# Four edits to a four-layer graph kernel: q and k stored whole and parted between the attention's steps, the nearest row taken in place, the norm rows on four row groups, h times the last weights ahead

## The chip, the core and the metric

The kernel runs on one core of one Trainium2 chip. Its time is the device time of one execution in microseconds (us). TensorE is called PE (PEld is its weight load), VectorE DVE, ScalarE ACT, GpSimd POOL; SP is the engine that here issues nearly all DMAs. L494 is line 494 of the kernel before.

## What is computed

x is 3327 x 128, adj a 3327 x 3327 matrix of zeros and ones (about 16 ones in a row). Each of four layers adds to x a function of h = relu(layernorm(x)):

```python
# layer 0: two rounds of message passing
x1 = swish((adj @ h) @ W + b);  out = swish((adj @ x1) @ W + b)
# layer 1: attention with 128 heads of 8 elements
q = (h @ Wq.T).reshape(128, n, 8); k, v likewise
a = softmax(einsum('dnh,dmh->dnm', q, k) * scale + adj + adj, axis=2)
out = einsum('dnm,dmh->dnh', a, v).reshape(n, 1024) @ Wo.T
# layer 2: a message and a GRU cell
out = gru(relu((adj @ h) @ W_msg.T + b_msg), h)
# layer 3: lap(A, y) = d * (A @ (d * y)) with d = 1/sqrt(row sums of A)
z = leaky_relu(lap(adj, h) @ W1 + b1, 0.1)
S = exp(-sqrt(squared distances of the rows of z) / 2)   # 4 largest of a row kept
out = lap(S + adj, h) @ W2 + b2
```

In `reshape(128, n, 8)` the flat index of a row's 1024 projected elements decides the head, so 26 consecutive rows of h hold one head.

## The kernel before, in words

Node n lies in partition n // 26 and slot n % 26 (T = 26 slots, 3327 = 128 x 26 - 1). The stages follow one another; outside the attention each engine's order is that of the program.

**Layer 0 (0 to 378 us).** Two products of adj, loaded from DRAM in 26 tiles, in float32.

**Projections (378 to 641 us).** For each of 26 blocks of 128 rows, PE forms q, k and v (L404, L415). ACT writes the rounded part of q and k (L409, `hi`, a type in which TensorE multiplies fast), DVE the rest (L410, `lo` = full - `hi`) and the largest magnitude (L411), and SP stores both parts to the DRAM tensors qt and kt (16 rows: 8 of `hi`, 8 of `lo`) and v to vd (L394). After block 1, `load_heads` issues the 28 loads of group 0.

**Attention (641 to 10,592 us).** The columns (queries) come in 7 chunks of 476, the heads in 32 groups of 4, the rows (keys) in 26 steps t. A step of a chunk and a group:

- PE multiplies k by q for four heads on four 32-row groups (L494). Even steps: three results for DVE ("early", 4 buffers), one for ACT ("late"). Odd steps: two and two. PE adds adj to the late ones (L497).
- DVE adds adj to each early one (L499) into p8, the tile of a pair of steps (3 buffers). ACT takes exponentials of the late ones (L500) and, at odd steps, of five results of both steps at once (L504). POOL multiplies one result by exp of adj at odd steps (L502).
- PE weighs v with the results of four steps earlier (L511). After a group DVE copies the sums out (L520) and SP stores them (L523).

At step 4 `load_heads` issues the loads of the next group's k, q and v: 8 of k (208 KB each, 16 partitions), 16 of q, 4 of v. From step 13 on, POOL casts one pair of key slots a step, 13 in all (`key_pair`, L373). At step 22 tiles of adj for the next chunk are loaded, doubled on POOL (L270) and stored as bfloat16. The order on every engine is the program's, under `manual_schedule`:

```python
scores(step, heads, a_t[t], e_t[t // 2], p8)
...
if j >= ahead:
    weigh(*begun.pop(j - ahead))
if t == min(4, T // 2) and more:
    coming = load_heads(*groups[n])
if t >= T // 2 and more:
    key_pair(coming)
```

**Output projection and layer 2 (10,592 to 10,856 us).** `adj_matmul_parts` (L228) multiplies adj in bfloat16 by three parts of y (its sum in bfloat16), 26 tiles of 21 matmuls; the tiles come through a pool of 4 that is opened for each product. Beside the first product PE transposes h (L646).

**Layer 3 (10,856 to 11,391 us).** A second product with adj gives z (L718 to L728). For each of 26 tiles PE forms the negative distances (L774) and adds the norms as products with K = 3 (L777: `one_rows` x `n_rows`, both on partitions 0 to 2), ACT evacuates (L778), DVE finds the eight largest (L779) and their indices (L780). `second` turns these, in pieces of 4, 9 and 13 tiles, into d2, weights `sim`, and y = h * d2 / 2, splits y and stores it to yd. A third product with adj runs beside the gathers: per tile POOL gathers four rows of yd (L791), DVE sums them by weight (L798, L800), PE transposes the sum (L805). At the end two float32 products with W2 per tile (L822, L823), two DVE operations per quad of tiles (L825, L826) and the stores (L829).

A flag n_gen, formed after the projections from the largest magnitudes and the low bits of adj, decides whether an exact and much slower version of the attention and of all that follows runs afterwards (`For_i` over n_once); for these inputs it is 0.

Of the kernel before, what the change touches and what calls it, by code (L numbers as in the profile page):

```python
# [8 lines left out]
F32 = mybir.dt.float32  # L9
F32R = mybir.dt.float32r  # L10
# [10 lines left out]
P = 128  # L21
# [5 lines left out]
E = 8  # L27
# [26 lines left out]
def kernel(  # L54
# [56 lines left out]
    deg = const.tile([P, T], F32, name="deg")  # L111
    a_max = const.tile([P, T], F32, name="a_max")
# [21 lines left out]
    def in_pieces(f):  # L134

        todo = [slice(t0, t1) for t0, t1 in zip(CUTS, CUTS[1:]) if t1 > t0]

        def done(t):
            while todo and todo[0].stop <= t:
                p = todo.pop(0)  # L140
                f(p, p.stop - p.start)

        return done
# [47 lines left out]
    def adj_matmul(agg, lhs, on_tile=None, bufs=3):  # L191

        cs = chunks(N, 512)
        with tc.tile_pool(name="adj_ps", bufs=1, space=PSUM) as ps, tc.tile_pool(name="adj_in", bufs=bufs) as ap:
# [23 lines left out]
    def adj_matmul_parts(agg, parts, on_tile=None):  # L218

        cs = chunks(N, 512)  # L220
        with tc.tile_pool(name="adj_ps", bufs=1, space=PSUM) as ps, tc.tile_pool(name="adj_in", bufs=4) as ap:
            acc = [ps.tile([P, 512], F32, name=f"agg_ps{c}") for c in range(len(cs))]
            for t in range(T):
                a = ap.tile([P, N], BF16, name="a16")
                nc.sync.dma_start(a, adj16[t])
                for i, part in enumerate(parts):
                    for c, (c0, w) in enumerate(cs):
# [5 lines left out]
                            stop=(t == T - 1 and i == 2),  # L233
# [39 lines left out]
    with tc.tile_pool(name="l0", bufs=1) as pool:  # L273
# [46 lines left out]
        fix = pool.tile([P, 1], F32, name="fix")  # L320
        nc.gpsimd.affine_select(fix, ones, pattern=[[0, 1]], compare_op=ALU.is_gt, fill=0.0, base=P - 1, channel_multiplier=-1)
        nc.vector.tensor_scalar(fix, fix, -1.0, 1.0, op0=ALU.mult, op1=ALU.add)
        nc.vector.tensor_add(deg[:, T - 1 : T], deg[:, T - 1 : T], fix)
# [4 lines left out]

    kt = dpool.tile([HL, GP], F32, name="kt")
# [15 lines left out]

    def load_heads(c, g):
        q0, _ = q_chunks[c]
        we = even(c)
        k_in = kq.tile([P, NP], F32, name="k_in", bufs=1)
        q4 = kq.tile([P, QW], F32R, name="q4")  # L350
        v4 = kq.tile([P, 4, T, EA], F32, name="v4")
        for i in range(4):
            n0 = (4 * g + i) * N
            for j in range(2):
                r = 32 * i + HL * j
                nc.sync.dma_start(k_in[r : r + HL], kt[:, n0 : n0 + NP])
                for k in range(2):
                    nc.sync.dma_start(
                        q4[r + E * k : r + E * k + E, :we].bitcast(F32),
                        qt[E * j : E * j + E, n0 + q0 : n0 + q0 + we],  # L360
                    )
# [14 lines left out]
    with tc.tile_pool(name="l1", bufs=1) as pool, tc.tile_pool(name="l1_ps", bufs=3, space=PSUM) as ps:  # L376
# [6 lines left out]
        for tail in (qt, kt):  # L383
            nc.gpsimd.dma_start(tail[:, N * NH :], zero)
# [12 lines left out]
        assert 3 * N + NP <= P * NH  # L397
        for r in range(T):
            kp = rows_of(r)
            lhs = hT[:, r * P : r * P + kp]  # L400
            for i, (dst, mx) in enumerate(((qt, q_max), (kt, k_max))):
# [3 lines left out]
                scale = D**-0.5 if i == 0 else 1.0  # L405
                s = st.tile([P, 2, E * NH], F32R, name="qk_st")
                full = pp[:kp].rearrange("p a b -> p (a b)")
                hi = s[:kp, 0].bitcast(F32)
                nc.scalar.activation(s[:kp, 0], full, AF.Copy, scale=scale)  # L409
                nc.vector.scalar_tensor_tensor(s[:kp, 1], full, scale, hi, op0=ALU.mult, op1=ALU.subtract)  # L410
                nc.vector.tensor_reduce(mx[:kp, r : r + 1], hi, AX.X, ALU.max, apply_absolute_value=True)  # L411
                store(dst.rearrange("e (r c) -> r e c", c=NH), s.bitcast(F32).rearrange("p a (e c) -> p (a e) c", c=NH), r, kp)
# [7 lines left out]
            if r == 1:  # L420
                first = load_heads(0, 0)
                while len(first[3]) < T // 2:
                    key_pair(first)
                e_first = [exp_of(a, 0) for a in a_first[1::2]]
# [15 lines left out]
        general = pool.tile([P, 1], F32, name="general")  # L440
# [515 lines left out]
```

## Time and profile before

| | |
|---|---|
| median of 3 runs | 11409.84 us (11403.6 to 11420.41) |
| the profiled execution, its span | 11392.72 us, 11391.0 us |
| PE, ACT, DVE, POOL busy | 97%, 90%, 83%, 50% of the span |
| granted PE clock, mean | 0.991 of full |
| DMA | 889.80 MB, 78 GB/s in the mean |
| attention, first L494 to last | 621.1 to 10,585.8 us |
| a group of the attention | 44.2 us (583 L500 in 990 us, one a step) |
| last add of the output (L826) ends | 11382.1 us |

A line of a group gives line, engine, operation, output<-input, shapes, count, busy us, mean ns of one, then the engine's idle time just before these instructions and what ended it. A line of a timeline gives start, length, engine, line, operation, and in brackets the idle time before it and its releaser. A line of windows gives, for a stretch, its length, the busy time of PE, PEld, DVE, ACT and POOL with their counts, then the granted PE clock, the DMA engines' share and GB/s. Instructions of one engine can overlap in the records, so a group's busy time may be less than count times mean.

### The profile page before, as it was taken

The numbers are of one execution on the slowest core, as the hardware profiler recorded it, in microseconds if no ns is written. First come the engines' busy times: TensorE is split into PE (matmuls) and PEld (weight loads), VectorE is DVE, ScalarE is ACT, GpSimd is POOL, SyncE is SP. The second block draws the span as 40 slices with busy tenths as digits, with TensorE's granted clock in tenths as the row PEclk, the third lists the DMA queues.
The fourth block names the chain that finished last, engine by engine and source line by source line (L and its number), as shares of the span: only waits on it lengthen the run. The fifth ranks groups of instructions, "written<-read, shape, count | busy, mean of one in ns | idle before, by whom it ended". The sixth has DMA issues, their size and how long they took to land. (4 is left out here: it accounts for less than half of the span.)

```text
span 11391.0 us, 212068 instructions
## 1 busy us (share of the span) xinstructions
PE 11065.1 (97%) x80100; PEld 3098.6 (27%) x80100; DVE 9408.1 (83%) x15508; ACT 10238.7 (90%) x9182; POOL 5727.5 (50%) x6218
## 2 busy tenths in 40 slices
PE   9789999999999999999999999999999999999998
PEld 4322222222222222222222222222222222222554
DVE  8678888888888888888888888888888888888555
ACT  0379999999999999999999999999999999999332
POOL 0135555555555555555555555555555555555103
PEclk9899999999999999999999999999999999999999
DMA  7853444444444444444444444444443434444423
GB/s 268 244 122 60 70 62 67 64 62 69 61 69 63 63 68 61 69 63 63 67 61 69 63 61 67 61 68 63 62 68 60 68 57 58 58 57 59 138 79 114
DMA packets 476579, 889.80 MB, mean 78 GB/s; under 512 B 91863, under 2 KB 423112, under 8 KB 439962
## 3 DMA queue, kind: packets, MB, share of 16 engines
q1 hardware_dynamic: 470952, 864.64, 43.5%
q8 instruction: 633, 10.37, 0.5%
q0 software_dynamic: 4592, 11.50, 0.3%
q14 instruction: 402, 3.29, 0.1%
HBM read 763.30 MB, written 112.46 MB: 77 GB/s over the span
## 5 line engine op out<-in xcount | busy, mean ns | idle before, releaser
L499 DVE TENSOR_TENSOR p<-early,a 128x476 f32<-128x476 f32 (+1 forms) x14560 | 8435.6, 644 | 1419.7 <-PE early L494 1192.3
L504 ACT ACTIVATE p<-p 128x2380 f32<-128x2380 f32 (+1 forms) x2912 | 6757.4, 2321 | 14.2 <-DVE p L499 0.5
L511 PE MATMUL acc<-p,v 128*9 128x476 f32 (+1 forms) x46592 | 5879.6, 564 | 33.4 <-POOL p L502 13.6
L502 POOL TENSOR_TENSOR p<-p,e 128x476 f32<-128x476 f32 (+1 forms) x2912 | 3539.2, 1215 | 3296.0 <-ACT p L500 3259.4
L500 ACT ACTIVATE p<-late 128x476 f32<-128x476 f32 (+1 forms) x5824 | 4529.2, 897 | 38.9 <-DMA vd<-v_st 20.3
L494 PE MATMUL early<-q,k 32*128 32x476 f32 (+1 forms) x14560 | 2882.9, 477 | 18.8 <-DVE p L499 18.8
L494 PE MATMUL late<-q,k 32*128 32x476 f32 (+1 forms) x8736 | 2797.3, 478 | 62.7 <-ACT p L500 36.3
L373 POOL CAST k<-k_in 128x256 fp32r<-128x256 f32 x2912 | 1946.7, 703 | 1162.5 <-DMA q<-qt 582.7
L494 PEld LDWEIGHTS late<-q,k 32*128 32x128 f32 x8736 | 1065.4, 181 | 4769.9 <-ACT p L500 3241.0
L497 PE MATMUL late<-a,two_i 128*128 128x476 bf16 (+1 forms) x5824 | 2181.0, 374 | 0.0
L494 PEld LDWEIGHTS early<-q,k 32*128 32x128 f32 x14560 | 1144.9, 181 | 23.9 <-DVE p L499 19.5
L511 PEld LDWEIGHTS acc<-p,v 128*9 128x9 f32 x46592 | 710.6, 88 | 1406.4 <-issue 1185.1
L497 PEld LDWEIGHTS <-two_i 128*128 128x128 bf16 x5824 | 556.3, 96 | 1327.5 <-issue 1327.5
L187 ACT COPY agg<-agg_ps 128x512 f32<-128x512 f32 x15 | 8.2, 590 | 476.7 <-PE agg_ps L201 289.7
L228 PE MATMUL agg_ps<-a,part 128*128 128x512 bf16 (+1 forms) x1638 | 338.0, 368 | 18.1 <-DMA a<-adj 13.7
L270 POOL TENSOR_SCALAR a<-a_in 128x476 bf16<-128x476 f32 (+2 forms) x156 | 222.2, 1424 | 0.5
L228 PEld LDWEIGHTS <-part 128*128 128x128 bf16 x1638 | 161.7, 99 | 188.6 <-DVE d_half L759 13.7
L409 ACT ACTIVATE qk_st<-pp 128x1024 fp32r<-128x1024 f32 (+1 forms) x52 | 53.3, 1024 | 149.0 <-DMA qt<-qk_st 67.4
L270 POOL TENSOR_SCALAR a<-a 128x476 bf16<-128x476 f32 (+1 forms) x26 | 36.4, 1400 | 295.3 <-DMA a<-in_adjT_dram 295.3
L778 ACT ACTIVATE dist<-sp,nsq 128x2048 f32<-128x2048 f32 (+1 forms) x52 | 85.5, 1647 | 109.8 <-PE sp L777 100.8
L774 PE MATMUL sp<-yT,hT 128*128 128x512 f32 (+1 forms) x364 | 168.2, 603 | 3.6 <-ACT hT L726 2.1
L201 PE MATMUL agg_ps<-a,h 128*128 128x512 f32 (+2 forms) x364 | 147.4, 568 | 24.3 <-DVE h L162 24.3
(192 smaller groups left out, 2520.2 us busy)
## 6 DMA issues: line engine op xcount, KB each, us to landing
k_in<-kt SPq DMA_DIRECT2D x1792, 208.0 KB
v<-vd SPq DMA_DIRECT2D x896, 117.0 KB
a<-in_adjT_dram SPq DMA_DIRECT2D x50, 1663.5 KB
a<-adj SPq DMA_DIRECT2D x78, 831.8 KB
q<-qt SPq DMA_DIRECT2D x3072, 14.9 KB
a_in<-in_adjT_dram SPq DMA_DIRECT2D x125, 238.0 KB
qt<-qk_st SPq DMA_DIRECT2D x25, 1024.0 KB
kt<-qk_st SPq DMA_DIRECT2D x25, 1024.0 KB
```

The costliest lines, as they stand in the source:

```text
L201: nc.tensor.matmul(acc[c][:, :w], lhs[:kp, t, :], a[:kp, c0 : c0 + w], start=(t == 0), stop=(t == T - 1))
L228: nc.tensor.matmul(acc[c][:, :w], part[:, t, :], a[:, c0 : c0 + w], start=(t == 0 and i == 0), stop=(t == T - 1 and i == 2),)
L270: nc.gpsimd.tensor_scalar(a2[:kp, :w], a, 2.0, None, op0=ALU.mult)
L373: nc.gpsimd.tensor_copy(k, slots(k_in)[:, t : t + 2, :])
L494: nc.tensor.matmul(sp[:, :we], pairs[t // 2][r, t % 2, :], q4[r, :we], start=True, stop=ways[i] != "I")
L497: nc.tensor.matmul(late[:, i - n_d, :we], two_i, a2[:, :we], start=False, stop=True)
L499: nc.vector.tensor_tensor(p8[:, places[i], :we], early[i][:, :we], a2[:, :we], op=ALU.add)
L500: nc.scalar.activation(p8[:, places[n_d] : places[3] + 1, :we], late[:, :, :we], AF.Exp)
L502: nc.gpsimd.tensor_tensor(p8[:, places[3], :we], p8[:, places[3], :we], e_a[:, :we], op=ALU.mult)
L504: nc.scalar.activation(p8[:, :5, :we], p8[:, :5, :we], AF.Exp)
L511: nc.tensor.matmul(acc[32 * i : 32 * i + EA, :w], v4[:kp, i, t, :], p8[:kp, PLACES[t % 2][i], :w], start=(t == 0), stop=(t == T - 1),)
L774: nc.tensor.matmul(sp[:, c0 : c0 + w], slots(zT)[:, t, :], z2T[:, cols], start=True, stop=False)
```

## The change

**q and k.** The projections store q and k whole, in float32, to qf and kf (8 rows each); `hi` and `lo` are no longer formed there. A new class `Parting` reads a group's q and k back (as 96 partitions of 1109), casts to `hi` on POOL in four pieces, subtracts on DVE in four pieces, and stores both to kt and qt. Groups 0 and 1 are parted between the blocks of the projections, with the first `load_heads`, the first exponentials and key casts spread over later blocks. Group g + 2 is parted during group g of the first chunk (c = 0; 30 groups): loads at step 0, k's casts at steps 5 to 8, each subtraction one step later, its stores at 11, q's casts at 15 to 18, its stores at 21. `hi` and each `lo` have one buffer. The loads of heads no longer read padding, which a memset writes instead.

**Nearest row in place.** Of a row's four nearest, the first is taken to be the row itself and is read from y in SBUF; three are gathered. Rows whose first nearest is another are found (`moved`), and n_gen, now formed at the end, is 1 if there is one.

**Norm rows.** `n_rows` and `one_rows` stand in four 32-row groups; the four 512-wide columns of a product use different ones.

**h times W2 ahead.** During the second product PE transposes h and multiplies it by W2; y becomes h W2 * d2 / 2, the weighted sums are added to x on DVE, and the end has one transpose per tile instead of two products. The adj tiles' pool is opened once for all three products, `second` has a last piece of 4 tiles, y is stored before it is split, and the distances' buffers are reused tiles.

```diff
@@ attention set-up
+    JW = 12
+    WJ = 4 * N // JW
+    W4 = -(-WJ // 4)
+    class Parting:
+        def rows(self, ap, r):
+            return dram(ap, r * GP + 4 * self.g * N, [[GP, E], [WJ, JW], [1, WJ]])
+        def load(self, side):
+            src, _, name = SIDES[side]
+            self.lo[side] = kq.tile([E * JW, WJ], F32R, name=name, bufs=1)
+            nc.sync.dma_start(self.lo[side].bitcast(F32), self.rows(src, 0))
+        def round(self, side, i):
+            if i == 0:
+                self.hi[side] = kq.tile([E * JW, WJ], F32R, name="hi", bufs=1)
+            p = slice(i * W4, min((i + 1) * W4, WJ))
+            nc.gpsimd.tensor_copy(self.hi[side][:, p], self.lo[side][:, p].bitcast(F32))
+        def rest(self, side, i):
...
+            nc.vector.tensor_sub(lo[:, p], lo[:, p].bitcast(F32), hi[:, p].bitcast(F32))
+        def store(self, side):
+            dst = SIDES[side][1]
+            nc.sync.dma_start(self.rows(dst, 0), self.hi[side].bitcast(F32))
+            nc.sync.dma_start(self.rows(dst, E), self.lo[side].bitcast(F32))
+        def steps(self):
+            todo = [(side, lambda side=side: self.load(side)) for side in range(2)]
+            for side, at in ((0, 5), (1, 15)):
+                for i in range(4):
+                    todo.append((at + i, lambda side=side, i=i: self.round(side, i)))
+                    todo.append((at + i + 1, lambda side=side, i=i: self.rest(side, i)))
+                todo.append((at + 6, lambda side=side: self.store(side)))
+            return sorted(todo, key=lambda due: due[0])
@@ projections
-                s = st.tile([P, 2, E * NH], F32R, name="qk_st")
-                nc.scalar.activation(s[:kp, 0], full, AF.Copy, scale=scale)
-                nc.vector.scalar_tensor_tensor(s[:kp, 1], full, scale, hi, op0=ALU.mult, op1=ALU.subtract)
+                s = st.tile([P, E * NH], F32, name="qk_st")
+                nc.scalar.activation(s[:kp], pp[:kp].rearrange("p a b -> p (a b)"), AF.Copy, scale=...)
...
-            if r == 1:
-                first = load_heads(0, 0)
-                while len(first[3]) < T // 2:
-                    key_pair(first)
-                e_first = [exp_of(a, 0) for a in a_first[1::2]]
+            if r > 1 and early:
+                early.pop(0)()
@@ attention, between load_heads and key_pair
+                if c == 0 and g + 2 < n_groups:
+                    if t == 0:
+                        parting = Parting(g + 2).steps()
+                    while parting and (parting[0][0] <= t or t == T - 1):
+                        parting.pop(0)[1]()
@@ layer 3, second product
-            adj_product(agg, y, parts)
+                adj_product(agg, y, parts, project_quad)
@@ distances
-                            nc.tensor.matmul(sp[:, c0 : c0 + w], one_rows, n_rows[:, cols], start=False, stop=True)
+                            r = slice(c0 // 16, c0 // 16 + 3)
+                            nc.tensor.matmul(sp[:, c0 : c0 + w], one_rows[r], n_rows[r, cols], start=False, stop=True)
@@ gathers
+                    if k == 0 and not general:
+                        row = y[:, t, :]
+                    else:
...
+                nc.vector.scalar_tensor_tensor(xs[:, t, :], g, d2[:, t : t + 1], xs[:, t, :], op0=ALU.mult, op1=ALU.add)
@@ output
-                        nc.tensor.matmul(op[:, j, :], slots(agg)[:, t0 + j, :], w2_s, start=True, stop=False)
-                        nc.tensor.matmul(op[:, j, :], gT[:, t0 + j, :], w2_s, start=False, stop=True)
+                        nc.tensor.transpose(op[:, j, :], slots(agg)[:, t0 + j, :], ident)
```

## The prediction

> **What bounds the kernel now.** First the attention stage (620 to 10,592 us, 87% of the span), by its groups of instructions in 663 to 1653 us, 22.4 of the 224 groups (count x, busy | idle before):
> ```profile
> L499 DVE TENSOR_TENSOR p<-early,a 128x476 f32<-128x476 f32 x1455 | 843.8, 645 | 136.0 <-PE early L494 115.4 <-ACT p L500 13.8 <-POOL p L502 3.9
> L504 ACT ACTIVATE p<-p 128x2380 f32<-128x2380 f32 x291 | 681.8, 2343 | 1.1
> L500 ACT ACTIVATE p<-late 128x952 f32<-128x952 f32 x583 | 459.8, 918 | 1.0 <-PE late L497 0.9
> L373 POOL CAST k<-k_in 128x256 fp32r<-128x256 f32 x292 | 195.2, 703 | 113.1 <-DMA q<-qt 61.5 <-DMA v<-vd 35.2 <-DMA a_in<-in_adjT_dram 11.5
> ```
> ACT idles 2.1 us in 990: it is the bound. A group (26 steps) lasts 44.2 us; DVE idles 136.0/22.4 = 6.1 us of it. POOL waits 5.05 us per group at its first key cast.
>
> Second, POOL's and DVE's timelines in one group (step 4 starts the loads of the next heads at 1005.6; step 13's scores are at 1018.3):
> ```profile
> 1020.89 1.21 POOL L502 TENSOR_TENSOR p<-p,e 128x476 f32<-128x476 f32 x1 [2.17 <-ACT p L500]
> 1027.74 1.34 POOL L373 CAST k<-k_in 128x256 fp32r<-128x256 f32 x2 [5.65 <-DMA v<-vd]
> 1029.05 1.20 POOL L502 TENSOR_TENSOR p<-p,e 128x476 f32<-128x476 f32 x1
> 1030.19 1.28 POOL L373 CAST k<-k_in 128x256 fp32r<-128x256 f32 x2
> ```
> ```profile
> 1007.36 2.89 DVE L499 TENSOR_TENSOR p<-early,a 128x476 f32<-128x476 f32 x5 [0.47 <-PE early L494]
> 1010.65 2.89 DVE L499 TENSOR_TENSOR p<-early,a 128x476 f32<-128x476 f32 x5 [0.39 <-ACT p L500]
> 1024.05 2.89 DVE L499 TENSOR_TENSOR p<-early,a 128x476 f32<-128x476 f32 x5 [0.50 <-PE early L494]
> ```
> POOL stands from 1022.1 to 1027.74 on key cast 13, since the heads take 22 us to land; L502 of step 15 runs 4.8 us late, and nobody minds. DVE's five adds (three of an even step, two of the odd one, 0.56 us apart) end at 1026.94, and ACT's L504 of that pair starts at 1027.17: DVE is only 0.2 us ahead of the bound.
>
> Third, the windows and SP's waits around the other stages:
> ```profile
> 430.00:618.00 188.00, 132.81 (x254) 48.88 (x255) 99.27 (x86) 63.24 (x63) 9.16 (x25) 0.92 1.04 300
> ```
> ```profile
> SPq L225 <- DVE idx L780: 83.4, 1, 83.4
> ```
> The projections of q, k, v are bound by DMA (share 1.04, 300 GB/s). The third adjacency product can't load until the distances end. After it the chain of waits follows the gathers:
> ```profile
> 11355.96 0.95 POOL row L791
> 11356.90 0.30 issue
> 11357.21 2.49 DMA row<-yd,idx
> ```
>
> **Projections: -70.** 188 us hold 21 blocks of 2,624 KB: 8.96 us each. A block now stores 1,600 KB, by bytes 5.46 us; PE's 12 matmul records of 0.43 make 5.13, so DMA still sets the pace: 26 x 3.5 = -91. Parting two groups moves 5.1 MB: +17. SP now stands at four stores behind a side's casts and subtractions (4 x 0.76 on POOL); DMA's backlog covers most, I take +4. The 20 us in which SP issues the first head loads (399.75 to 420.90) remain, only later. Ends: -85 (packets of 512 B cost more per byte) and -50 (each stand in full).
>
> **Attention, 30 groups of chunk 0: +190.** Per group come eight casts of 96x278 on POOL (2.75 ns a column from L373: 0.76 us, 6.1 in all, in POOL's 44% idle), eight subtractions on DVE (L214: 655 ns for 512 columns, 1348 for 1152; so 0.40, 3.2 in all, below its 6.1 idle) and six DMAs of 426 KB; DMA has room (share 0.00 from 1030 to 1040). By shares this is free. By order it is not: an engine runs in order, and a subtraction is queued one step after its cast.
>
> Side 0 (casts at steps 5 to 8). L502 of step 5 ends at 1008.55, the cast at 1009.31; DVE finished its three adds of step 6 at 1009.05, waits, subtracts, and the two adds of step 7, which L504 needs, end 0.66 us late: ACT loses 0.6. Again at step 8; at odd steps the subtraction fits DVE's gap of 0.4. Sum 1.2.
>
> Side 1 (casts at 15 to 18). Its first cast is queued behind key casts 13 and 14 and L502: 1027.74 + 1.31 + 1.20 + 0.76 = 1031.0. DVE is at its subtraction at 1025.74, with the adds of step 17 and all later ones queued behind it; PE then waits for DVE's PSUM buffers, ACT for the adds. They end near 1032.5 instead of 1026.9: L504 5.4 us late, less the 1.2 by which steps already lag the loads: 4.2. At step 18 the cast stands behind two key casts, another cast and L502, ready at 1035.0 against 34.7: 0.6. Sum 4.8.
>
> A port may add to this. L721 on 256 columns, with two SBUF inputs, took 1.14 us beside a POOL product that ended at 10994.90; L720 of that width took 0.42:
> ```profile
> 10993.58 0.42 DVE L720 TENSOR_TENSOR ln_xc<-ln_xc,b_s 128x256 f32<-128x256 f32 x1
> 10994.03 1.14 DVE L721 SCALAR_TENSOR_TENSOR ln_xc<-ln_xc 128x256 f32<-128x256 f32 x1
> ```
> L499 reads PSUM and one SBUF tile; the subtraction reads two SBUF tiles, and POOL is busy with the next cast or key when it comes. Holding for one such op (0.65 to 0.76) at four even steps gives side 0 2.6, side 1 3.5 + 1.3: 7.4 instead of 6.0. The mean key wait (5.05 for 5.65) takes 0.5 off both. I take 6.5, nearer the row with the port: 30 x 6.5 = 195, less 5 for 0.17 us per group that ACT loses already. Ends 3.5 (heads 2 us earlier) and 9.
>
> The Trainium skill ("SBUF — State Buffer", section "SBUF: two separate sides") states that a VectorE instruction with two SBUF inputs and a GpSimd one that reads SBUF take turns on a shared port pair, the first holding it for its whole length. The trace shows this once, in L721; if the rule holds every time, the term is +202, and without it +160.
>
> The clock can add. After the hole at 621 to 641 us an attention step takes 2.92 us at a granted clock of 0.50 (649.74 to 652.66), against 1.64 at 1.00. PE's hole here is some 3.7 us; one of 2.5 at 10803 left the clock up, slices with 2.4 to 3.3 of 4 us busy at 438 to 450 were followed by 0.50. Two cold steps are +2.6; hence the 9. The skill's page "TensorE: Matmul & The Clock Gate", section "What's actually happening", halves the clock only after a whole idle window of about 3.4 us, free-running; by it this hole would seldom do so and the term stays at +190, by the rows of 438 to 450, which show 0.50 without such a window, it goes to +265.
>
> **Later chunks and small edits: 0.** Pad memsets on POOL (0.13 us, L267) lie in its idle time; if not, 0.13 a group, 29 in all. SP waits 5,146 us for L520, which covers the six issues.
>
> **Tail: -34.** (a) h times W2 goes into the second product, where PE is busy 112.4 of 116.8 us: 26 transposes (L646: 4.1/26 = 0.16) and 26 products (L718: 12.5/26 = 0.48): +16.6. (b) Distances: PE sets 7.81 us per tile; the K=3 products take 0.96 + 0.65 of it. In the attention four matmuls on four 32-row groups end together in 0.48, so some 0.7 goes, and DVE becomes the bound: 3.63 + 0.09 + 3.62 = 7.35, -0.46 x 26 = -12, with four pieces' small DVE operations back on the path +4: -8 (0 if they don't overlap). (c) The distances end at 11214.85 = D. The gathers began at D + 11.8; the last piece now has 4 tiles (y 0.69 for 1.89 us, split behind the store): d_half at D + 4.1, y at 4.8, and 3.7 for 256 KB to land where 832 KB took 5.8: D + 8.5. 78 gathers of 0.945 + 0.30 instead of 104, with 1.3 for the slow first and 2.5 for landing, end at D + 110, not D + 145. PE needs 26 x 4.33 (11324.75 to 11329.08) = 112.6 from D - 7 (tiles prefetched; before, PE idled 13.3 for them): D + 105, hidden. Evacuation 2.2, then 26 transposes under DVE's 7 x 1.35 instead of 18.5 us of products: last add D + 123 against D + 167. The flag's reduction (POOL 0.39, four DVE operations of 0.15) is inside the 9 us from the last add to the span's end, else +1: -43.
>
> **Sum.** The profiled run took 11392.7 us (span 11391.0), 17.1 below the median of 11409.8. -70 + 190 - 34 = +86: 11479 in its terms, 11496 as a median. About 23 us (0.2%) is what a measurement can tell from no change.
>
> **Rivals.**
> *DVE isn't held* (faster): the subtractions fall into its 6.1 us. Only side 0's 1.2 is paid: +36 - 104 = -68: 11342. For it: DVE 86%, POOL 56% busy. Against: 5.05 us of POOL's wait in every group. It decides when a group loses under 104/30 = 3.5 us, that is, when the heads land over 2 us sooner. Chance 0.18.
> *Hole and cold clock* (slower): the hi buffer of side 0 is stored behind the head loads on the same queue, lands after 1030, and PE restarts at 0.50: 9 us a group, +270 - 104 = +166: 11576. Chance 0.16.
> *Projections don't shrink*: SP's stands and 512-B packets leave -50 there and -20 in the tail: 11530. Chance 0.08.
> *It doesn't do what it says*: if some row's nearest isn't itself, the exact loop runs and a whole attention stage comes on top, over 20,000. Chance 0.01.
> The forecast has the remaining 0.57, range 11440 to 11550. Faster takes the first rival, 0.18; 0.05 of the forecast's low edge is within 0.2%; slower 0.77. The range that holds 8 in 10 reaches half into the first rival and past the second: 11345 to 11590.
>
> **What would show it.** Right: in chunk 0 groups of some 50.5 us against 44.2; one DVE gap near 5 us per group released by a POOL cast, and the same gap before L504; chunks 1 to 6 unchanged; projections near 190 us to the first exponential, against 263; gathers 78 and the last add 123 us after the distances. Wrong: ACT without gaps in chunk 0, or casts that run ahead of the keys.

## The result, and the profile after

The change takes 11588.5 us (median of 4 runs, 11580.1 to 11591.7) where the kernel before takes 11406.7 (median of 4, 11397.2 to 11420.4): a ratio of 1.0157, with a 95% interval of 1.014 to 1.0175, so 182 us slower. Forecast were +86 and 11496, with a range of 11345 to 11590: the side was right, the size not. The profiled execution took 11586.8 us (span 11585.1).

The stages of the two profiled executions, each cut at the same event in both traces, against the terms of the forecast:

| stretch | before | after | difference | forecast |
|---|---|---|---|---|
| start to the first exponential of the attention loop | 644.0 | 574.1 | -70 | -70 |
| chunk 0 (32 groups) | 1427.2 | 1631.1 | +204 | +190 |
| chunks 1 to 6 | 8521.1 | 8533.7 | +13 | 0 |
| end of chunk 6 to the distances' end (D) | 622.5 | 631.6 | +9 | +16.6 - 8 |
| D to the last add | 166.8 | 199.5 | +33 | -43 |
| last add to the span's end | 9.4 | 15.1 | +6 | 0 to 1 |

Unrounded they sum to +194, the difference of the two spans. Three terms stand, as sums, as they were worked out, one is 14 us short, and one, the end of the kernel, has the wrong sign. The +13 of the later chunks lies within the spread: two executions of the kernel before differ by 29 there (8521.1 in the profile of before, 8491.8 in before_again below). Whether the change has a part in it, no run shows.

**Attention, chunk 0.** The groups of instructions in 663 to 1653 us, as shown of before:

```profile
L558 DVE TENSOR_TENSOR p<-early,a 128x476 f32<-128x476 f32 x1262 | 736.8, 643 | 87.4 <-PE early L553 78.7 <-ACT p L559 7.0 <-PE late L556 1.0
L563 ACT ACTIVATE p<-p 128x2380 f32<-128x2380 f32 x252 | 555.8, 2206 | 96.2 <-DVE p L558 91.4
```

In the same 990 us ACT makes 252 of its wide exponentials (L563, L504 before) instead of 291: 51.1 us a group against 44.2. It idles 96.2 us before them where it idled 1.1, and what ends that idle time is DVE. One group of the timelines of POOL, DVE and ACT shows how (L376 is the cast, L381 the subtraction, L427 the key cast):

```profile
1001.69 1.21 POOL L561 TENSOR_TENSOR p<-p,e 128x476 f32<-128x476 f32 x1 [2.18 <-DMA k_in<-kt]
1008.23 1.26 POOL L427 CAST k<-k_in 128x256 fp32r<-128x256 f32 x2 [5.33 <-DMA v<-vd]
1009.45 1.19 POOL L561 TENSOR_TENSOR p<-p,e 128x476 f32<-128x476 f32 x1
1010.58 0.41 POOL L376 CAST hi<-lo_q 96x278 fp32r<-96x278 f32 x1
```
```profile
1004.85 1.77 DVE L558 TENSOR_TENSOR p<-early,a 128x476 f32<-128x476 f32 x3 [0.49 <-PE early L553]
1011.03 1.23 DVE L381 TENSOR_TENSOR lo_q<-lo_q,hi 96x278 fp32r<-96x278 f32 x1 [4.41 <-POOL hi L376]
1012.18 1.20 DVE L558 TENSOR_TENSOR p<-early,a 128x476 f32<-128x476 f32 x2
1013.30 0.96 DVE L381 TENSOR_TENSOR lo_q<-lo_q,hi 96x278 fp32r<-96x278 f32 x1
1017.75 0.43 DVE L381 TENSOR_TENSOR lo_q<-lo_q,hi 96x275 fp32r<-96x275 f32 x1
```
```profile
1013.41 2.19 ACT L563 ACTIVATE p<-p 128x2380 f32<-128x2380 f32 x1 [5.03 <-DVE p L558]
```

POOL stands 5.33 us on a key cast until the head loads land; the cast of the second side is behind it and ends at 1010.99. DVE's subtraction waits 4.41 us for it, the two adds that the exponential needs are behind the subtraction, and ACT waits 5.03.

TensorE (PE) stands idle for that time too, and the clock granted to it falls. Its first row after the hole, ACT's row of the next step, and the six microseconds from 1010 as a window (PE, PEld, DVE, ACT and POOL busy us, instructions in brackets; then the granted clock, DMA share and GB/s):

```profile
1012.88 0.76 PE L553 MATMUL early<-q,k 32*128 32x476 f32 x1 [4.80 <-DVE p L558]
```
```profile
1017.10 0.96 ACT L559 ACTIVATE p<-late 128x952 f32<-128x952 f32 x1 [1.04 <-PE late L556]
```
```profile
1010.00:1016.00 6.00, 3.12 (x14) 0.73 (x14) 4.97 (x8) 2.58 (x2) 6.00 (x10) 0.61 0.15 58
```

The clock records of the trace have 0.50 for 6.8 us in each of 29 groups, and in chunk 0 of the kernel before and of e4_early only in its first 10 us. The step behind the hole takes PE 2.90 us (1012.88 to 1015.78) for 1.64, and ACT waits for it. By the starts of ACT's wide exponentials, in the mean of 28 groups and beside the kernel before, the wait adds 4.85 us to a group, the two steps behind it 1.18 and 0.38, and the first side 0.53: 6.9 us in all.

**The end of the kernel.** Windows of the third product, in the same columns:

```profile
11375.00:11395.00 20.00, 20.00 (x102) 9.78 (x100) 6.94 (x21) 2.22 (x4) 12.05 (x13) 1.00 0.67 220
11395.00:11415.00 20.00, 4.89 (x14) 1.20 (x12) 9.07 (x29) 0.00 (x0) 15.13 (x17) 0.66 0.20 53
11415.00:11435.00 20.00, 3.89 (x7) 0.73 (x7) 4.80 (x15) 0.00 (x0) 12.88 (x15) 0.50 0.29 89
11495.00:11515.00 20.00, 20.00 (x101) 9.76 (x100) 0.00 (x0) 0.00 (x0) 0.00 (x0) 1.00 0.62 202
```

The product starts as forecast at D - 7.8 and runs at about 100 matmuls in 20 us. From 11396 us, 16 us after the first gather (11380.0), it makes seven in 20 us, later up to thirteen, until the gathers end; then it runs at full rate again. TensorE's timeline in between, and its weight loads':

```profile
11397.29 0.27 PE L232 MATMUL agg_ps<-a,part 128*128 128x255 bf16 x1 [0.97 <-issue]
11399.39 0.38 PE L232 MATMUL agg_ps<-a,part 128*128 128x512 bf16 x1 [1.83 <-issue]
11402.20 0.58 PE L232 MATMUL agg_ps<-a,part 128*128 128x512 bf16 x1 [2.44 <-issue]
```
```profile
11398.69 0.10 PEld L232 LDWEIGHTS <-part 128*128 128x128 bf16 x1 [2.65 <-issue]
11400.78 0.10 PEld L232 LDWEIGHTS <-part 128*128 128x128 bf16 x1 [2.00 <-issue]
```

One instruction starts 0.7 or 1.4 us after the other, weight load and matmul in turn, and the profile names nothing that they wait for. The waits of 11190 to 11560 us (sum, times, longest) show DVE touched too:

```profile
PEld L232 <- issue: 93.3, 54, 2.7
PE agg_ps L232 <- issue: 69.6, 43, 2.4
DVE g L907 <- remote: 25.5, 13, 2.4
```

Below this is called the crawl. It makes the product 196 us long instead of some 110, and the last add comes at D + 200 instead of D + 123. The DMA share is low in it (0.16 to 0.32), the gathers keep one per 1.25 us for most of it. The crawl comes and goes between sets of runs of one and the same program (e4_early and e9_again below), and several numbers below can't be read without knowing whether a run had it.

### The profile page after: what moved, and what is told of

Read it like the earlier page. It is cut to its first block, busy times and chain, and to the rows that moved or that the text cites. A ratio compares the mean times of both kernels' runs of the same rounds, so it can differ in the third digit from the quotient of the medians.

```text
span 11585.1 us, 213018 instructions
## 1 busy us (share of the span) xinstructions
PE 11120.0 (96%) x80074; PEld 3109.3 (27%) x80074; DVE 9505.1 (82%) x15764; ACT 10254.2 (89%) x9163; POOL 5839.8 (50%) x6710
## 4 chain that ended last, share of the span: by engine, by line
PE 71%; DMA 11%; DVE 8%; issue 4%; ACT 2%; POOL 2%; SPq 1%; DVEq 0%; POOLq 0%; ACTq 0%
PE acc L570 35%; PE late L553 16%; PE late L556 11%; DMA q<-qt 6%; DVE p L558 5%; DMA k_in<-kt 3%; PE agg_ps L232 3%; PE agg_ps L205 2%; PE early L553 1%; ACT p L559 1%; DMA v<-vd 1%; DVE o L579 1%; POOL p L561 1%; SPq L582 1%; PE pp L470 1%
## 5 line engine op out<-in xcount | busy, mean ns | idle before, releaser
L563 ACT ACTIVATE p<-p 128x2380 f32<-128x2380 f32 (+1 forms) x2912 | 6703.2, 2302 | 161.9 <-DVE p L558 141.1
L559 ACT ACTIVATE p<-late 128x476 f32<-128x476 f32 (+1 forms) x5824 | 4480.6, 879 | 77.4 <-PE late L556 66.4
L553 PE MATMUL early<-q,k 32*128 32x476 f32 (+1 forms) x14560 | 2928.4, 479 | 138.3 <-DVE p L558 138.2
L427 POOL CAST k<-k_in 128x256 fp32r<-128x256 f32 x2912 | 1954.6, 704 | 1176.3 <-DMA q<-qt 545.5
L381 DVE TENSOR_TENSOR lo_q<-lo_q,hi 96x278 fp32r<-96x278 f32 (+1 forms) x128 | 101.0, 792 | 121.4 <-POOL hi L376 121.4
L579 DVE COPY o<-acc 105x476 f32<-105x476 f32 (+1 forms) x224 | 143.9, 642 | 4.6 <-PE acc L570 4.6
```

The costliest lines, as they stand in the source:

```text
L427: nc.gpsimd.tensor_copy(k, slots(k_in)[:, t : t + 2, :])
L553: nc.tensor.matmul(sp[:, :we], pairs[t // 2][r, t % 2, :], q4[r, :we], start=True, stop=ways[i] != "I")
L559: nc.scalar.activation(p8[:, places[n_d] : places[3] + 1, :we], late[:, :, :we], AF.Exp)
L563: nc.scalar.activation(p8[:, :5, :we], p8[:, :5, :we], AF.Exp)
L579: nc.vector.tensor_copy(o4[: 96 + EA, :w], acc[: 96 + EA, :w])
```

## The experiments

Three sets of four and two of three; the kernels of a set ran on one chip, beside runs of the kernel before. "Last add" is its start after the distances' end D, from the trace. Each time is one run, but for three of set 4: the kernel before (median of 8), after_again (of 4) and e6_again (of 5).

| set | kernel before, us | kernel: us, last add |
|---|---|---|
| 1 | 11398 | e1_flag 11580, D + 202; e2_pool 11584, + 202; e3_gathers 11600, + 233; e4_early 11387, + 201 |
| 2 | 11366 | e6_tails 11310, + 131; e7_sums 11320, + 126; e8_dummy 11318, + 124 |
| 3 | 11365 | e9_again 11320, + 124; e10_act 11322, + 125; e11_pe 11324, + 124; e12_place 11322, + 122 |
| 4 | 11406 | after_again 11574, + 201; before_again 11393, + 199; e6_again 11349, + 161; e7_again 11402, + 206 |
| 5 | 11380 | after_third 11522, + 124; e13_pause 11374, + 168; e14_tie 11344, + 124 |

### What makes DVE wait: e4_early

```
-    hi = kq.tile(..., name="hi", bufs=1)
+    hi = kq.tile(..., name="hi", bufs=2)
-    for side, at in ((0, 5), (1, 15)):
+    for side, at in ((0, 4), (1, 9)):
-    k = kq.tile(..., name="k", bufs=T)
+    k = kq.tile(..., name="k", bufs=T - 4)
```

> The change with one edit in the attention stage: the casts of the first side are at steps 4 to 7 and those of the second side at steps 9 to 12 instead of 15 to 18 (with two hi buffers and 22 instead of 26 key buffers, for space), so that POOL makes all of them before its key casts wait for the heads. Theory as predicted (of the 6.8 us that a group of chunk 0 loses, most is DVE's subtraction queued behind a cast that stands behind the key casts): DVE's gap near 4.4 us goes, a group falls from 51 to some 46.5 us, 30 x 4.5 = 135 us gained, time near 11453. Rival (DVE's own time, 8 subtractions of 0.43 to 1.23 us, is what costs): a group stays at 49 us or more, time 11530 to 11590.

Measured: 11386.8 us, 200 less than the change, with the same tail (crawl, D + 201). Chunk 0 lasts 1439.8 us, 191 less; the groups of 663 to 1653 us:

```profile
L558 DVE TENSOR_TENSOR p<-early,a 128x476 f32<-128x476 f32 x1443 | 841.3, 643 | 78.4 <-PE early L553 67.1 <-POOL p L561 3.9 <-ACT p L559 2.7
L563 ACT ACTIVATE p<-p 128x2380 f32<-128x2380 f32 x289 | 645.6, 2234 | 3.9
```

ACT makes 289 wide exponentials and idles 3.9 us: 44.5 us a group. It was the place of the second side in POOL's row. (The edit also moves the first side by a step and gives `hi` a second buffer; that POOL waited for the heads, and not for `hi`, is what its timeline above shows, and the first side cost 0.5 us a group.) The same eight casts and eight subtractions, made before the key casts, cost a chunk 13 to 18 us in 30 groups (1439.8 against 1427.2 and 1421.9): the rival, DVE's own time, is out. The gain was even larger than expected, as the subtractions became shorter too: 434 ns in the median against 636 for the second side before.

### Three guesses at the crawl: e1_flag, e2_pool, e3_gathers

The loop count formed from the bound alone:

```
+        nc.vector.tensor_copy(n_gen, unsafe)
...
-                nc.vector.tensor_reduce(need, moved, AX.X, ALU.max)
-                nc.gpsimd.partition_all_reduce(need, need, P, bass_isa.ReduceOp.max)
-                nc.vector.tensor_max(need, need, unsafe)
-                nc.vector.tensor_copy(n_gen, need)
```

> The change with one edit: the loop count n_gen is formed from the bound alone right after the projections, as before, so that the comparison of the nearest row with the own row no longer feeds it, and POOL's all-reduce and SP's read of the flag are not between the distances and the gathers. (The check that each row is its own nearest is left out.) Theory F (the flag's chain, which stands directly ahead of the first gather in the order, is what makes the third product crawl at 1.4 us per PE instruction from 11396 to 11490 us): no crawl, the last add comes some 123 us after the distances' end instead of 200, the time is 11589 - 77 = 11512. Theory R (PE started before the gathers, at full rate from prefetched tiles) and theory G (three gathers a tile and the row in place): the crawl stays, 11580 to 11595. The attention stage is untouched in both.

Each product's adjacency tiles from a pool of its own:

```
-    with tc.tile_pool(name="adj_ps", ...) as ps:
+    with tc.tile_pool(name="adj_ps", ...) as ps, tc.tile_pool(name="adj_in", bufs=4) as pool:
```

> The change with one edit: the a16 tiles of each adjacency product come from a pool of their own that is opened at the product, as before, so the third product's tiles are loaded only after the distances have given their space back. Theory R (a product that starts 17 us before the gathers at full rate is what is new, and crawls): the third product starts some 13 us later and then runs beside the gathers without a crawl, some 113 us long; last add about 136 us after the distances' end instead of 200, time near 11525; the second product is a little later too (a few us at most). Theory F (the flag): the crawl stays, its start moved by some 13 us; 11585 to 11600.

The nearest row gathered again:

```
-                    if k == 0 and not general:
+                    if False:
```

> The change with one edit: the nearest row is gathered again (four gathers a tile, 104 in all), nothing is taken in place. Theory G (the crawl comes from three gathers a tile with DVE's operations close behind each): no crawl; gathers end 104 x 1.25 = 130 us after the first, about 142 us after the distances' end, last add some 160 us after it instead of 200, time near 11550. Theories F and R: PE crawls to the end of the gathers, which is 26 x 1.25 = 32 us later: a few more matmuls get through, and the time is 11610 to 11625.

The crawl is in all three (D + 202, + 202, + 233). It begins 15 to 16 us after the first gather, when TensorE has made 157, 162 or 181 matmuls, and ends 1 to 3 us after the last; 104 gathers make it 31 us longer. So theories F and G don't hold. Theory R was not tried: e2_pool's edit didn't put the product off. SP loaded its first four tiles at 11131 to 11133 us, long ahead of D, and it began at D - 7.8, as in the change. What speaks against R is the kernel before in set 4, whose product begins at D + 4.5, 7 us ahead of its gathers, and crawls.

### What TensorE, ACT and DVE do beside the gathers: e6 to e8, e9 to e12

e6_tails takes the sums out of the loop as before (transposes on TensorE, copies on ACT, a second product at the end); e7_sums leaves only DVE's add out; e8_dummy keeps the add and puts transposes and copies back. The core of e6_tails:

```
-                nc.vector.scalar_tensor_tensor(xs[:, t, :], g, d2[:, t : t + 1], xs[:, t, :], ...)
+                gs.append(g)
+            def transpose_gathered(t):
+                tp = g_ps.tile([P, P], F32, name="tp")
+                nc.tensor.transpose(tp, gs[t], ident)
+                nc.scalar.copy(gT[:, t, :], tp)
+            def beside(t):
+                gather(t)
+                if t >= LAG:
+                    transpose_gathered(t - LAG)
...
-                        nc.tensor.transpose(op[:, j, :], slots(agg)[:, t0 + j, :], ident)
+                        nc.tensor.matmul(op[:, j, :], slots(agg)[:, t0 + j, :], ident, start=True, stop=False)
+                        nc.tensor.matmul(op[:, j, :], gT[:, t0 + j, :], ident, start=False, stop=True)
```

> e4_early with the gathered sums taken into the end of the tail as before: TensorE transposes each tile's sum (six tiles late) between the tiles of the third product, ACT copies it, and the end adds it through a second product; DVE's add into xs beside the product (L908) is gone. Theory W (TensorE crawls where nothing in its stream waits for the gathers; before, one transpose a tile tied it to them) or theory X (DVE's add into xs of each tile makes it crawl): no crawl, third product and gathers side by side in some 115 us, last add about 125 to 135 us after the distances' end instead of 200: near 11387 - 68 = 11319. Theory D (something of the changed distances or of the earlier parts does it): the crawl stays, 11380 to 11410.

> e4_early with DVE's add into xs of each tile (L908) taken out from beside the third product: the sums stay in a tile of their own and are added at the end, four tiles at a time. TensorE's stream is that of the change, with nothing in it that waits for the gathers. Theory X: no crawl, 11387 - 75 + 7 x 0.7 = 11317. Theories W and D: the crawl stays, 11385 to 11400.

> e4_early with the transposes of the gathered sums on TensorE and their copies on ACT put back beside the third product, their results not used, and DVE's add into xs kept. Theory W: no crawl, last add some 125 to 135 us after the distances' end, 11387 - 68 = 11319. Theories X and D: the crawl stays, and since each transpose then stands in it the time is 11385 to 11410.

No crawl in any of them, which no single theory had foreseen, and a kernel before of 11366 instead of 11398, on the chip of set 1. So the next set began with a control: e4_early, unchanged.

In e10_act the copies stand without the transposes, in e11_pe the transposes without the copies; in e12_place the sums have a tile of their own:

```
-                g = gpool.tile([P, D], F32, name="g")
+                g = gsum[:, t, :]
```

> e4_early once more, on the chip of the next three. If the crawl of the third product belongs to the program, it is here again: last add some 200 us after the distances' end, and the time is within 15 us of the kernel before. If it belongs to the chip of the runs above (theory C: the chip or its state), there is none, the time is some 75 us below the kernel before.

> e4_early with one copy a tile on ACT beside the third product (of the sum of six tiles before, its result not used), and no transposes on TensorE. Theory A (the crawl needs an ACT that stands idle, as it does in the change; before, it copied once a tile): no crawl, 75 us below e9_again. Theory W (it needs a TensorE that never waits for the gathers) and theory X (DVE's add into xs): the crawl stays, within 15 us of e9_again.

> e4_early with one transpose a tile on TensorE of the sum of six tiles before, and no copies on ACT (one at the end; the results are not used). Theory W: no crawl, 70 us below e9_again. Theories A and X: the crawl stays, within 20 us of e9_again.

> e4_early with the sums in a tile of their own for all 26 (as in e7_sums) and DVE's add into xs kept beside the product (unlike e7_sums). Theory X: the crawl stays, within 15 us of e9_again. Theory B (what e7_sums cured was the eight buffers of the sums, whose reuse makes DVE's first operation of a tile wait for the add of an earlier one): no crawl, 75 us below e9_again.

The control has no crawl either. Two windows of the same program 20 us after the first gather, e4_early of set 1 and e9_again of set 3:

```profile
11200.00:11220.00 20.00, 4.01 (x8) 0.72 (x7) 8.25 (x25) 0.00 (x0) 15.13 (x16) 0.53 0.21 52
```
```profile
11210.00:11230.00 20.00, 19.89 (x100) 9.70 (x100) 7.74 (x26) 0.00 (x0) 15.12 (x17) 1.00 0.74 245
```

POOL and DVE do the same in both; TensorE makes 8 matmuls or 100. The program doesn't decide whether the crawl comes, and sets 2 and 3 say nothing on A, B, W and X. Theory C holds but for its price: e9_again was 45 below the kernel before, not 75, since the kernel before was itself 33 faster.

### The change and the kernel before with the crawl and without: set 4, and after_third

> The change itself, once more. In all runs on record it took 11580 to 11592 us beside a kernel before of 11397 to 11420; e4_early differed by 67 us between two sets of runs, with the crawl in one and without it in the other, and the kernel before by 33 (11398 and 11365). Theory C1 (the crawl comes and goes with the chip's condition at the time, not with the program): where the kernel before takes some 11365 the change has no crawl and takes 11587 - 77 = 11510 to 11525; where the kernel before takes some 11400 it crawls and takes 11580 to 11592. Theory P (the crawl belongs to the change): 11580 to 11592 in either case.

> The kernel before itself, for its trace in the condition of this chip. If it takes some 11365, its trace shows beside that of 11392.7 where the 27 to 33 us lie: theory C2, that the same condition slows the kernel before in its tail too, beside the gathers, has them between the distances' end and the last add (167 us there, then some 135); the rival has them in the attention stage, spread over 224 groups (0.1 us each). If it takes some 11395, nothing is learnt but its spread.

> e6_tails once more (the moved casts, and the gathered sums transposed beside the product and added by TensorE at the end). Where the kernel before takes 11365: 11310, 0.995 of it, with an interval that stays below 1. Where it takes some 11400, this tells what the crawl needs: if the program has a part in it (one transpose a tile that ties TensorE to the gathers, no add into xs), no crawl and some 11315 to 11345; if not, 11380 to 11390.

> e7_sums once more (the moved casts; DVE's add into xs out of the loop, TensorE not tied to the gathers). Where the kernel before takes 11365: 11320. Where it takes some 11400: if the add into xs is what the crawl needs, 11320; if a TensorE that is not tied to the gathers is, 11385 to 11395.

In set 4 the crawl was there, in the kernel before too. Its TensorE timeline:

```profile
11218.40 0.59 PE L228 MATMUL agg_ps<-a,part 128*128 128x512 bf16 x1 [2.34 <-issue]
11221.20 0.37 PE L228 MATMUL agg_ps<-a,part 128*128 128x255 bf16 x1 [2.22 <-issue]
11252.02 5.29 PE L228 MATMUL agg_ps<-a,part 128*128 128x512 bf16 x14 [0.31 <-issue]
```

From 11213, 18.7 us after its first gather, it crawls at the same pace, and from 11249 on speeds up again. Its last add is at D + 199, against D + 167 in the profile of before: theory C2's 32 us are there. That its total (11392.8) equals that of the profile of before (11392.7) is chance: it reached D 32 us sooner (11182.7 for 11214.8), by a shorter attention stage. So the profile from which the prediction was made is the one without the crawl, and no line of it could show it.

e6_again lost 30 us (D + 161 for D + 131), e7_again all of it (D + 206). The timelines of e6_again, POOL, TensorE, ACT and DVE in turn, show the moment at which its crawl ends:

```profile
11211.05 0.94 POOL L901 DMA_INDIRECT row<-yd,idx  x1 [0.30 <-issue]
11218.17 0.94 POOL L901 DMA_INDIRECT row<-yd,idx  x1 [6.17 <-DVE g L910]
```
```profile
11195.52 0.37 PE L232 MATMUL agg_ps<-a,part 128*128 128x255 bf16 x1 [1.66 <-issue]
11217.54 0.47 PE L915 MATMUL tp<-ident,g 128*128 128x128 f32 x1 [21.65 <-ACT ln_sq L916]
```
```profile
11217.22 0.27 ACT L916 COPY ln_sq<-tp 128x128 f32<-128x128 f32 x1 [43.74 <-remote]
```
```profile
11217.22 0.29 DVE L908 TENSOR_SCALAR g<-y,sim 128x128 f32<-128x128 f32 x1 [13.32 <-remote]
```

TensorE had made the transpose that ACT waits for at 11184.10; ACT learns of it at 11217.22, and DVE of its free buffer in the same instant. So it is not only TensorE's own instructions that are late but its signals to the others. By then the gathers had stood still for 5.2 us: TensorE waits for ACT's copy, DVE for TensorE's buffers and POOL for DVE's, so POOL has nothing to issue after 11212. In before_again the same pause comes ahead of the speeding up at 11249:

```profile
11258.02 0.94 POOL L791 DMA_INDIRECT row<-yd,idx  x1 [12.47 <-DVE g L798]
```

POOL's last gather ahead of it ended at 11245.5. In the change the last gather of all started at 11486.0, and TensorE is at full rate from 11489.9. So theory J for the last set: the signals come through some 3 to 5 us after the last gather's end, and a kernel in which nothing makes the gathers pause keeps the crawl to the end.

One trace of the set doesn't fit. In e7_again POOL's last gather ends at 11285.6, and TensorE crawls on to 11297.8, 12.2 us longer, while DVE, ACT, POOL and the DMA engines stand nearly still:

```profile
11289.00:11293.00 4.00, 1.16 (x2) 0.17 (x2) 0.00 (x0) 0.00 (x0) 0.00 (x0) 0.50 0.01 4
```

So the crawl can outlast the gathers, and how long a pause it needs to end is not known.

> The change itself a third time. Where the kernel before takes some 11365 (the condition without the crawl): no crawl, last add 123 us after the distances' end and 11495 to 11515, so that its cost beside the kernel before is 130 to 150. Where the kernel before takes some 11400: 11575 to 11592 again.

> e4_early with a slow stretch in POOL's row of gathers: after the 27th, five products of 128x3328 that nothing uses stand between the next gathers, some 7 us each. Theory J (the crawl is a jam that the gathers at one per 1.25 us keep up, and that clears when they pause, as in before_again and e6_again): where the crawl is there, it begins some 16 us after the first gather and ends within the slow stretch; the last add comes some 150 us after the distances' end. Rival (the crawl lasts as long as gathers run): it lasts through to the last gather, 35 us later than in e4_early, last add near 235 us after the distances' end. Where there is no crawl: last add at 145 to 155 us.

> e11_pe once more: one transpose a tile on TensorE of the gathered sum of six tiles before, so that the sums' buffers, and with them DVE and the gathers, wait for TensorE when it crawls. Theory J: where the crawl is there, it ends by itself after some 20 to 40 us, when the gathers have run out of buffers; last add some 160 us after the distances' end and 11350 to 11360. Rival (the tie does nothing, what e6_again gained came from leaving out the add into xs or from ACT): 200 us and 11385 to 11400. Where there is no crawl: 11320 to 11325.

Set 5 came without the crawl, so e13_pause and e14_tie say nothing on J, which rests on traces of set 4, with e7_again against its 3 to 5 us, and on no edit; e13_pause's slow stretch was also dearer than expected (D + 168, not 145 to 155). The edit of e13_pause:

```
+                if t == 8:
+                    nc.gpsimd.tensor_mul(idle, y, over_f(row, T))
+                    for _ in range(4):
+                        nc.gpsimd.tensor_mul(idle, idle, y)
```

after_third gives the change without the crawl: 11521.7 beside 11380.4, +141, with a window some 45 us after the distances' end of

```profile
11425.00:11445.00 20.00, 20.00 (x102) 9.80 (x101) 8.19 (x27) 0.00 (x0) 15.33 (x16) 1.00 0.75 238
```

the product from D - 7.8 to D + 101.9 and the last add at D + 123.8.

**A version that beats both.** e6_again, with the moved casts and the sums tied to TensorE, took 11349.3 us (median of 5) beside 11405.8 of the kernel before: a ratio of 0.9957, interval 0.9942 to 0.9971, with the crawl; without it one run each gave 11309.8 and 11366.1.

## Why the prediction was right in its side and wrong in its size

- **Projections, -70: right** as a sum (69.9 by the first exponentials of the loop); its terms were not tried one by one.
- **Attention, +190 (measured +204): the wait was right, the other parts were not, and that the sum came near is partly luck.** The place and the length of the wait were those of the forecast: a gap of 4.41 us on DVE for 5.0 worked out, 5.03 on ACT, and 4.85 a group for the 4.8 of the second side. Two terms were mis-sized with opposite signs. The first side, put at 2.6 with the port, cost 0.53. The cold clock, kept for the end of the range, came in each of the 29 groups, and the two steps behind the hole cost 1.56. Sum 6.9 for 6.5. e4_early takes wait, hole and cold clock away together: 191 of the 204 go when the second side is cast ahead of the key casts.
- **Why the clock was left out.** The forecast reads a hole of 2.5 us at 10803 that left the clock up. That row was misread: no matmul runs there for 1.17 us (10804.56 to 10805.72), and holes of 2.3 and 2.4 us in the same profile, at 10687.9 and 10854.0, are followed by 0.50 (from 10691.6 and 10855.4). The holes of the change (2.8 to 5.5 us, median 4.5) were followed by 0.50 in 29 groups of 29.
- **The port: right in kind, on the wrong side.** In the second side L381 took 1.23 and 0.96 us beside a busy POOL and 0.43 without it, an excess of 0.5 to 0.8 for the 0.65 to 0.76 counted. The Trainium skill ("SBUF — State Buffer", section "SBUF: two separate sides") has the two engines take turns for a whole instruction when DVE has two SBUF inputs and GpSimd reads SBUF; the rows agree. But the forecast's extra 1.4 us stood in the first side, whose four subtractions took 0.43 to 0.53 in that group.
- **h times W2 and the distances, +16.6 - 8: right** (+9 together; from the second product's first matmul to the first one of z 112.9 us became 128.5, and from the first distance product to D 216.8 became 207.7).
- **End of the kernel, -43: the step that failed.** That PE needs 26 x 4.33 = 112.6 us from D - 7, ends at D + 105 and so is hidden behind the gathers, holds in after_third and e9_again (109.7 us, D + 101.9; last add D + 124 for the forecast D + 123). In the profiled run of the result the product took 196 us instead, for the crawl: the last add came 77 us late. (The other three runs of the result took as long in all; they have no trace.) The forecast had read the gathers and the product side by side at full rate in the one profile of before, and took a single profiled execution for what such an overlap costs. It had no rival in which they hinder each other.
- **The base.** The crawl costs the kernel before some 32 us and the change 77, as the change took away the transposes by which a slow TensorE had made the gathers pause. That is read from the traces of set 4 (two kernels with the tie, two without) and not shown by a single edit, since e14_tie met no crawl.
- **Sum.** With the crawl in neither, the profile of after_third is 129 us longer than that of before, for 86 forecast: -72 to the first exponential, +204 in chunk 0, +22 in chunks 1 to 6, +14 from there to D, -43 to the last add, +4 behind it. Beside the kernel before of its own set it is 141, by one run each. With the crawl in the change it is 182 (whether the kernel before's four runs had it, no trace shows) and, in set 4, 168 (after_again, 1.015, interval 1.0133 to 1.0167).
- **Behind the last add, 0 to 1 (measured +4 to +6).** POOL's closing DRAIN lasts 8.07 us in the change, and 8.07 to 8.16 in every kernel here with three gathers a tile; it lasts 1.30 in the kernel before and in e3_gathers, which have four. In e3_gathers 8.6 us lie between last add and end, in the change 15.2. Why the drain is longer is open.

Of the rivals, half of the second came: the hole and the cold clock, at 6.9 us a group and not 9, and behind the wait for the casts, not behind `hi`'s store. DVE was held, the projections shrank, and the exact loop didn't run. What causes the condition stays open, and that a pause of the gathers ends a crawl was seen but not tried. It isn't one chip, since sets 1 and 2 had the same; it isn't the flag, the number of gathers or the row in place (set 1, with the crawl in each).

## What to carry to other kernels

Work that is moved onto an idle engine in small steps costs what stands ahead of it in that engine's row, not its own time: place a step whose result a busy engine waits for ahead of the instruction that waits for a transfer, and ask for every cross-engine wait what else is queued behind the waiter. An overlap that a single profile shows at full rate can have another price in the next set of runs: where a term of the forecast rests on two engines running freely side by side, profile the kernel before more than once, and keep both ends. Before an edit is blamed or praised, run the same program again in the set that is to decide.

## What the runs showed of the hardware that was not expected

- Beside software gathers (0.94 us each on POOL, one per 1.25 us) TensorE can fall to one instruction per 0.7 or 1.4 us, from 15 to 19 us after the first gather on, and its signals to ACT and DVE can come up to 33 us late (once, in e6_again), until 1 to 12 us after the gathers pause or end. It was there in two sets of five and in the profiled run of the result, and in set 4 in the kernel before as in the change.
- In the crawl the granted clock was 0.50 with no gap over 1.4 us between TensorE's instructions, weight loads counted (11408 to 11490 us), at a busy time of 3.9 to 6.7 us in 20. In chunk 0 it fell with up to 0.74 us of matmuls, once 1.26, in the 3.4 us ahead of the fall. The Trainium skill ("TensorE: Matmul & The Clock Gate", section "What's actually happening") halves the clock after an idle window of about 3.4 us; here a window with sparse work in it was enough, and the measurement decides.
- The 29 stretches at 0.50 in chunk 0 begin 51.20 us apart, as long as a group then lasts (51.2 in the mean).
- Four products of three rows on four row groups ended together in 0.39 us (1.03 before).
